# First loads on one queue, fillings by 0.7 of the wait, output transfers as steps of the plan, and new ranks in a two-layer attention kernel

## The chip, the cores and the metric

The kernel runs on one core of a Trainium2 chip. Its engines work side by side, each from its own queue of instructions in order: TensorE (matmuls; PE, and PEld for its weight loads), VectorE (DVE), ScalarE (ACT), GpSimd (POOL) and SyncE (SP), which only issues transfers. ScalarE and GpSimd can issue transfers too. Engines wait for one another by semaphores. The metric is the device time of one execution in microseconds; lower is better.

## The reference

`x` is 16 batch elements of 256 tokens and 256 features; `ctx` is 16 elements of 77 tokens. The first layer is a transformer block, the second a pair of attentions round a very narrow mlp (4 hidden units). All is float32.

```python
# layer 0: 16 heads of 16 features
h = rmsnorm(x, sa_w);   h = x + attention(h, h, sa_wq, sa_wk, sa_wv, sa_wo)
hn = rmsnorm(h, ca_w);  h = h + attention(hn, ctx, ca_wq, ca_wk, ca_wv, ca_wo)
hn = rmsnorm(h, mlp_w); h = h + (silu(hn @ w_gate) * (hn @ w_up)) @ w_down     # 256 -> 1024 -> 256

# layer 1: one head
nX, nF = layernorm(ctx, n1w, n1b), layernorm(h, n2w, n2b)
a = softmax(nF @ nX.T * 256 ** -0.5) @ nX
c = gelu(a @ fc1_w.T + fc1_b) @ fc2_w.T + fc2_b                                 # 256 -> 4 -> 256
n = layernorm(c, n3w, n3b)
out = nF + gamma2 * (c + gamma1 * (softmax(n @ n.T * 256 ** -0.5) @ n))
```

## The kernel before

A batch element's 256 tokens are two tiles of 128 partitions. Elements are loaded and stored in pairs (`UB = 2`, buffers `h`), the context in pairs too (`cx` for layer 0, `cx2` for layer 1). The work of one element is written as generators, one for each stage: `self_operands` (rmsnorm, feature-major copy, projections `psq`, `psk`, `psv`), `self_maxima` (scores `sc`, row maxima, their transposes `tm`), `exponentials` (scores again, transposed, as `st`, then the exponential `pT`), `outputs` (`po`), `projection` (`wo`), the same for the cross attention (`cross_queries` with `pscq`, `csc`, `cst`, `cpo`, `cwo`; `cross_keys` with `tpc` for a pair), `mlp` (`pg`, `pu`, `wd`), `second_context` and `second` for layer 1. Scores use TensorE in row groups of 32 partitions (shape "r"), attention outputs and `lav` in column groups of 32 (shape "c"), the rest the full array ("f").

To get features onto partitions, the first pair transposes on TensorE (`tp_sa`, `tp_ca`, `tp_mlp`). Later elements transpose blocks of 32 on VectorE (`hb`, L429), write them to DRAM (`blocks`, L434) and read them back re-arranged (`hnT`, L439); both transfers are issued by SyncE.

The order is written out by a planner at build time. Every generator yields `Step`s: TensorE's time (`pe`), its shape, the work of other engines that follows (`ops`), what it needs, which buffers it takes and frees, and a `lag`, the time by which what it gives becomes ready after it. `Order` holds a clock for each engine. In each turn `start` (L263) tells for each stream the earliest time of its next step. Among TensorE steps the one with the smallest key is chosen: first those that are not late, then by rank, which is the batch number plus a constant of the stage (`RANKS`, L1234; the second number is added for the first two elements, the third for the last three), plus a penalty for a change of shape (`STANDS_BACK`, L235) and for the wait. Steps without TensorE are put in between when they fit. `put` then makes the generator emit the instructions, so the order of the calls is the order in every engine's queue. Times of loads are given as constants (`order.done`, L1227).

When the chosen TensorE step starts later than TensorE's clock, `keep_busy` (L326) puts fillings there: `idle` matmuls of the identity on itself, in the shape of the moment, whose output is not used. Their number comes from the planned wait and `T_IDLE`; the first ones (`FIRST_IDLE`) stand at the start of the kernel.

The head of the kernel is issued in plain order before the plan: `h` of the first pair in four tiles (L102 to L105) with the context in between, then GpSimd's identity and the two halves of `sa_nw`, then on ScalarE's queue `wq`, `wk`, `wv` (two transfers each) and `wo`, and on SyncE's the second pair, the cross weights, the mlp weights (L156 to L165), the later pairs and the small constants of layer 1 (`second_constants`, L874). The weights `wq`, `wk`, `wv`, `cwq`, `wg`, `wu` are then multiplied by their norm's weights in place (L1209). The store of a finished pair (L1192) is issued right behind VectorE's last addition (L1191), whose step is also what frees the buffer of `h` in the plan.

## Time and profile before

| what | value |
|---|---|
| time, median of 3 runs | 997.14 us (995.62 to 997.92) |
| time of the profiled execution | 996.82 us |
| its span, first to last instruction | 995.0 us |
| mean granted TensorE clock | 0.989 |
| VectorE, ScalarE, GpSimd busy | 63%, 48%, 9% of the span |
| transfers | 39.61 MB, mean 40 GB/s; 275 GB/s in the first fortieth of the span |
| waits of TensorE, the three longest in sum | `tp_sa` for ScalarE 2.6 us, the first `idle` 2.5 us, `pscq` for the read-back of `hnT_ca` 2.4 us |
| SyncE waiting for VectorE's last addition before a store | 123.6 us, 8 times |

The span is the time between the first and the last instruction; 1.8 us of the profiled execution's time lie outside. "Busy" for TensorE has modelled ends, and fillings count as busy, so the share says that TensorE always had something to do, not that it was useful. Two records stand for one float32 matmul, for the matmul and for its weight load alike. A line of the timeline has start, duration, engine, source line, operation, what is written and read, and in brackets how long the engine was idle before and what ended it. In the table of stretches PEclk is the share of TensorE's full clock that was granted. Line numbers are those of the kernel before.

### The profile page before, as it was taken

Reading aid. Unit: us, or ns where it says so; the run is one execution under the profiler, and the core shown is the slowest. Engines: PE = TensorE matmul, PEld = TensorE weight load, DVE = VectorE, ACT = ScalarE, POOL = GpSimd, SP = SyncE. Lnnn points to the kernel's source line nnn. Section 1 sums busy time; section 2 is a strip of 40 time slices with the busy share of each in tenths; the row PEclk is TensorE's granted clock in tenths of the full one; section 3 lists DMA queues with packets and bytes.
Section 4 is the critical chain, followed back from the end, with each engine's and each line's share of the span. In section 5 each row is a group of like instructions: output and inputs, shape, how many; then the busy total and the mean of one; then the engine's idle time right before and its main releaser. Section 6 shows DMA issues by size and latency. Waiting matters only on the chain.

```text
span 995.0 us, 18977 instructions
## 1 busy us (share of the span) xinstructions
PE 968.8 (97%) x8136; PEld 715.0 (72%) x8136; DVE 622.7 (63%) x1075; ACT 475.7 (48%) x770; POOL 93.7 (9%) x124
## 2 busy tenths in 40 slices
PE   7989999999999999999999999999999999999997
PEld 6766666676776667777776777777677777778876
DVE  4865576666675657766676655775578565655552
ACT  4246645334555364543755354454571526543432
POOL 2510000000010010100100000010020000100210
PEclk9899999999999999999999999999999999999997
DMA  8301001001000111002100121011210110001000
GB/s 275 82 24 39 22 11 40 2 22 32 29 23 22 42 61 43 12 33 77 43 12 22 46 83 46 1 33 35 64 54 1 49 33 23 32 12 54 12 22 22
DMA packets 45732, 39.61 MB, mean 40 GB/s; under 512 B 4336, under 2 KB 39760, under 8 KB 45648
## 3 DMA queue, kind: packets, MB, share of 16 engines
q1 hardware_dynamic: 44448, 37.34, 11.8%
q8 instruction: 64, 1.05, 0.4%
q10 hardware_dynamic: 1136, 1.05, 0.3%
q14 instruction: 20, 0.16, 0.1%
q0 software_dynamic: 64, 0.00, 0.0%
HBM read 23.14 MB, written 15.20 MB: 39 GB/s over the span
## 4 chain that ended last, share of the span: by engine, by line
PE 86%; DMA 4%; DVE 4%; ACT 4%; issue 1%; ACTq 0%; POOL 0%; SPq 0%; POOLq 0%
PE pg L828 11%; PE pu L828 11%; PE wd L858 11%; PE sc L574 6%; PE st L635 6%; PE po L677 5%; PE cst L635 3%; PE psq L499 3%; PE pscq L499 3%; PE wo L716 3%; PE cpo L677 3%; PE cwo L716 3%; PE psk L499 3%; PE psv L748 2%; PE csc L600 2%; ACT pT L643 2%
## 5 line engine op out<-in xcount | busy, mean ns | idle before, releaser
L579 DVE TENSOR_REDUCE nmax<-sc 128x8 f32<-128x2048 f32 x64 | 146.6, 2290 | 39.3 <-PE sc L574 39.2
L643 ACT ACTIVATE pT<-st 128x2048 f32<-128x2048 f32 x64 | 120.1, 1877 | 100.9 <-PE st L635 100.7
L828 PE MATMUL pg<-hnT_mlp,wg 128*128 128x256 f32 x512 | 129.8, 387 | 0.0
L828 PE MATMUL pu<-hnT_mlp,wu 128*128 128x256 f32 x512 | 128.7, 387 | 0.5 <-DVE sg L839 0.5
L858 PE MATMUL wd<-wd,gT 128*128 128x256 f32 x512 | 126.3, 388 | 0.0
L828 PEld LDWEIGHTS pu<-hnT_mlp,wu 128*128 128x128 f32 x512 | 93.4, 190 | 22.9 <-issue 10.6
L858 PEld LDWEIGHTS wd<-wd,gT 128*128 128x128 f32 x512 | 92.6, 190 | 23.8 <-issue 11.9
L828 PEld LDWEIGHTS pg<-hnT_mlp,wg 128*128 128x128 f32 x512 | 92.6, 190 | 21.0 <-issue 9.5
L643 ACT ACTIVATE cpT<-cst 77x2048 f32<-77x2048 f32 x32 | 59.9, 1872 | 59.2 <-PE cst L635 59.2
L838 ACT ACTIVATE sg<-pg 128x512 f32<-128x512 f32 x64 | 38.2, 597 | 101.5 <-PE pg L828 101.3
L839 DVE SCALAR_TENSOR_TENSOR sg<-sg,pg 128x512 f32<-128x512 f32 x64 | 43.9, 686 | 67.2 <-ACT sg L838 66.7
L677 PE MATMUL po<-pT,vone 128*32 128x256 f32 x1024 | 62.7, 382 | 0.1
L840 DVE SCALAR_TENSOR_TENSOR gT<-sg,pu 128x512 f32<-128x512 f32 x64 | 43.7, 683 | 28.5 <-PE pu L828 27.4
L607 DVE TENSOR_REDUCE nmax<-csc 128x16 f32<-128x1232 f32 x32 | 46.1, 1440 | 8.3 <-PE csc L600 8.0
L677 PEld LDWEIGHTS po<-pT,vone 128*32 128x32 f32 x1024 | 29.7, 109 | 26.0 <-issue 9.7
L210 POOL TENSOR_TENSOR rstd_n<-ve_n,neg_half 128x4 f32<-128x4 f32 (+3 forms) x28 | 23.4, 837 | 206.2 <-DVE ve_n L208 160.6
L210 POOL TENSOR_TENSOR rstd_ca<-ve_ca,neg_half 128x2 f32<-128x2 f32 x16 | 11.1, 697 | 304.7 <-DVE ve_ca L208 304.6
L335 PE MATMUL idle<-ident 128*128 128x128 f32 (+2 forms) x198 | 32.5, 327 | 2.5 <-POOL ident masks.py:199 2.5
L499 PE MATMUL pscq<-hnT_ca,cwq 128*128 128x256 f32 x128 | 31.7, 388 | 2.4 <-DMA hnT_ca<-blocks_ca 2.4
L499 PE MATMUL psk<-hnT_sa,wk 128*128 128x256 f32 x128 | 33.4, 397 | 0.0
L499 PE MATMUL psq<-hnT_sa,wq 128*128 128x256 f32 x128 | 33.4, 399 | 0.0
L335 PEld LDWEIGHTS idle<-ident 128*128 128x128 f32 (+2 forms) x198 | 30.7, 228 | 3.5 <-POOL ident masks.py:199 2.5
(614 smaller groups left out, 1570.8 us busy)
## 6 DMA issues: line engine op xcount, KB each, us to landing
h<-in_x_dram SPq DMA_DIRECT2D x7, 512.0 KB
blocks_sa<-hb_sa SPq DMA_DIRECT2D x14, 256.0 KB
hnT_sa<-blocks_sa SPq DMA_DIRECT2D x14, 256.0 KB
blocks_ca<-hb_ca SPq DMA_DIRECT2D x14, 256.0 KB
hnT_ca<-blocks_ca SPq DMA_DIRECT2D x14, 256.0 KB
blocks_mlp<-hb_mlp SPq DMA_DIRECT2D x14, 256.0 KB
hnT_mlp<-blocks_mlp SPq DMA_DIRECT2D x14, 256.0 KB
out_dram<-h SPq DMA_DIRECT2D x7, 512.0 KB
```

The lines of the kernel that those rows point to most:

```text
L335: nc.tensor.matmul(ps[cols, :P], lhsT=ident[rows, cols], rhs=ident[rows], start=True, stop=True)
L499: nc.tensor.matmul(ps[:, m * n : (m + 1) * n], lhsT=w[:, c, m * P : (m + 1) * P], rhs=src(c), start=(c == 0), stop=(c == NC - 1),)
L574: nc.tensor.matmul(sc[:, j, (1 - e) * S : (2 - e) * S], lhsT=a.qx[rg, c, e, qt * P : (qt + 1) * P], rhs=a.kx[rg, c, e], start=True, stop=True,
L579: nc.vector.tensor_reduce(maxima_of(nm, qt)[:, :, c::NC], sc.rearrange("p j (y k) -> p j y k", y=2), AX.X, ALU.max, negate=True,)
L607: nc.vector.tensor_reduce(maxima_of(nm, qt), sc[:, :, : 2 * NC * SK].rearrange("p j (n k) -> p j n k", k=SK), AX.X, ALU.max, negate=True,)
L635: nc.tensor.matmul(st[:nk, j, e * S : (e + 1) * S], lhsT=a.kx[rg, c, e, kc * P : kc * P + nk], rhs=a.qx[rg, c, e], start=True, stop=True,)
L643: nc.scalar.activation(a.pT[k][:nk].rearrange("p j e q -> p j (e q)"), st[:nk], AF.Exp, scale=HD ** -0.5,)
L677: nc.tensor.matmul(po[RG * j : RG * (j + 1), e, :], lhsT=a.v[:nk, kc, 8 * c + 2 * j + e, :], rhs=pT[:nk, j, e, :], start=(kc == 0 and e == ...
L716: nc.tensor.matmul(ps[:, i * D : (i + 1) * D], lhsT=oT[:, c, i * P : (i + 1) * P], rhs=a.w[:, c, :], start=(c == 0), stop=(c == NC - 1),)
L828: nc.tensor.matmul(ps[:, i * S : (i + 1) * S], lhsT=w[:, c, (f + i) * P : (f + i + 1) * P], rhs=tokens_moving(hnT, c), start=(c == 0), sto ...
L839: nc.vector.scalar_tensor_tensor(sg, sg, 1.0, ps, ALU.add, ALU.mult)
L858: nc.tensor.matmul(ps[:, :D], lhsT=gT[:, f, i * P : (i + 1) * P], rhs=wd[:, f, :], start=(f == 0), stop=(f == NF - 1),)
```

## The change

The four tiles of the first pair, the context, `sa_nw`, `wk`, `wv` and `wo` are issued on SyncE in the order in which they are used; of the first weights `wq` alone stays on ScalarE. The fillings' number is 0.7 of the planned wait less 150 ns, over `T_IDLE`, from one filling up (before: the wait less 350 ns, from two up), and 9 instead of 12 at the start. A TensorE step is late from a wait of 200 ns (100), a wait weighs 0.003 per ns in its rank (0.05), late ones go by their start alone, and leaving row or column groups for the full array costs 50 ranks (5). Steps of SyncE that would begin after TensorE's clock are set aside until TensorE's clock has passed them or nothing else is left; other steps may run 800 ns past the chosen TensorE step (500). The store of a finished pair is a step of SyncE of its own, and the buffer of `h` is free 3 us after it. The planned times of first loads and contexts are new, and so are most of the `RANKS`.

```diff
-    for t in range(NT):
-        if t == QT:
-            cxs[0] = load_context(0, UB, "cx")
-        load_tokens(0, t)
...
+    for t in range(QT):
+        load_tokens(0, t)
     ident = const.tile([P, P], F32, tag="ident", name="ident")
     make_identity(nc, ident)
-    sa_nw = load_columns(sa_norm_w, "sa_nw", nc.gpsimd, True)
+
+    wq = load_matrix(sa_wq, "wq", nc.scalar, True)
+    sa_nw = load_columns(sa_norm_w, "sa_nw", nc.sync, True)
+    wk = load_matrix(sa_wk, "wk", nc.sync, True)
+    wv = load_matrix(sa_wv, "wv", nc.sync, True)
+    for t in range(QT, NT):
+        load_tokens(0, t)
+    cxs[0] = load_context(0, UB, "cx")
+    wo = load_matrix(sa_wo, "wo", nc.sync)
...
-    wq = load_matrix(sa_wq, "wq", nc.scalar, True)
-    wk = load_matrix(sa_wk, "wk", nc.scalar, True)
-    wv = load_matrix(sa_wv, "wv", nc.scalar, True)
-    wo = load_matrix(sa_wo, "wo", nc.scalar)
     load_tokens(1)
...
-    T_IDLE, FIRST_IDLE = 220, 12
+    T_IDLE, FIRST_IDLE = 220, 9
-    STANDS_BACK = {"rf": 5, "cf": 5, "fc": 10}
+    STANDS_BACK = {"rf": 50, "cf": 50, "fc": 10}
...
-            n = int((t - self.clock["P"] - 350) / T_IDLE) if self.clock["P"] else FIRST_IDLE
-            if n < 2 or None in bank + after or max(bank + after) > self.clock["P"]:
+            n = int((0.7 * (t - self.clock["P"]) - 150) / T_IDLE) if self.clock["P"] else FIRST_IDLE
+            if n < 1 or None in bank + after or max(bank + after) > self.clock["P"]:
                 return
...
-                        late = wait > 100
-                        rank = st.rank[0] + STANDS_BACK.get(turn, 0) + 0.05 * wait
-                        key = (late, t + T_TURN[turn] if late else 0, rank, st.rank[1])
+                        late = wait > 200
+                        rank = st.rank[0] + STANDS_BACK.get(turn, 0) + 0.003 * wait
+                        key = (late, t if late else 0, rank, st.rank[1])
...
-                        aux.append((max(t + T_NEXT, self.clock[e]), st.rank, st, t))
+                        b = max(t + T_NEXT, self.clock[e])
+
+                        (ahead if e == "S" and b > self.clock["P"] else aux).append(
+                            (b, st.rank, st, t)
+                        )
+                if not best and not aux:
+                    aux = ahead
                 if aux:
                     b, _, st, t = min(aux, key=lambda a: a[:2])
-                    if best is None or b + sum(o[1] for o in st.step.ops) <= best[2] + best[1].step.pe + 500:
+                    if best is None or b + sum(o[1] for o in st.step.ops) <= best[2] + best[1].step.pe + 800:
...
-        yield Step(460, "r", "sc", ops=[("V", 70 + 290 * NT)], rel=[("h", u)] * (first + nb == UB),
-                   gives=[("second", n)])
+        yield Step(460, "r", "sc", ops=[("V", 70 + 290 * NT)], gives=[("second", n)])
         nc.vector.tensor_tensor(h, h, by_rows(zT, k["last"], "out"), ALU.add)
+        yield Step(ops=[("S", 600)], rel=[("h", u)] * (first + nb == UB), lag=3000)
         nc.sync.dma_start(tokens(out, u)[:, first * QT : first * QT + NT], h)
...
     def context_loads():
...
-                ops=[("S", 100)], acq=[("cx", u)], gives=[("cx", u)], lag=4000 if u else 6000
+                ops=[("S", 100)], acq=[("cx", u)], gives=[("cx", u)], lag=(8000, 20000)[u] if u < 2 else 4000
...
     def second_loads():
...
-            yield Step(ops=[("S", 100)], acq=[("cx2", u)], gives=[("cx2", u)], lag=4000)
+            yield Step(ops=[("S", 100)], acq=[("cx2", u)], gives=[("cx2", u)], lag=4000 if u > 1 else 20000)
...
-        ("x", 0): 5e3, ("x", 1): 20e3, "wq in": 8e3, "wk in": 9e3, "wv in": 10e3, "cwk": 12e3,
+        ("x", 0): 4e3, ("x", 1): 20e3, "wq in": 5e3, "wk in": 6e3, "wv in": 7e3, "cwk": 12e3,
...
     RANKS = {
...
-        "outputs": (6.5, -1, 50),
-        "exponentials": (-52.5, -50, 4),
-        "projection": (-0.5, -50, -0.5),
-        "cross_outputs": (5, 0, 0.25),
-        "cross_exponentials": (-100, 0, 0),
-        "cross_projection": (-50.5, 0, 50),
-        "self_maxima": (-0.25, -50, -100),
-        "cross_maxima": (-49, 0, 0),
-        "cross_queries": (-2, 1, -49.5),
-        "self_operands": (-2, 0, -0.5),
-        "cross_keys": (1.75, 0, 0),
-        "mlp": (4.25, 2.75, -2.5),
-        "second_context": (5.5, 0, -50),
-        "second": (3, 0, -50),
+        "outputs": (5.5, -1, 50),
+        "exponentials": (-51.5, -50, 5),
+        "projection": (0.5, -50, 3.5),
+        "cross_outputs": (-45, 0, 0.25),
+        "cross_exponentials": (-50, -50, 0),
+        "cross_projection": (-51.5, 0, 50),
+        "self_maxima": (0, -50, -50),
+        "cross_maxima": (-50, 0, -50),
+        "cross_queries": (-1, -52, 0.5),
+        "self_operands": (0, 0, -50.5),
+        "cross_keys": (2.25, 0, 48),
+        "mlp": (5, -0.25, 47.5),
+        "second_context": (-44.5, 0, 0),
+        "second": (-48, -1.5, -50),
```

More of the change, by code (lines that the diff above doesn't have):

```diff
@@ L342, in run @@
                 best = None
-                aux = []
+                aux, ahead = [], []
                 for st in self.streams:
```

## The prediction

> **What bounds the kernel now.** I read the page first: shares, then the 40 slices.
>
> ```profile
> PE 968.8 (97%) x8136; PEld 715.0 (72%) x8136; DVE 622.7 (63%) x1075; ACT 475.7 (48%) x770; POOL 93.7 (9%) x124
> PE   7989999999999999999999999999999999999997
> PEclk9899999999999999999999999999999999999997
> ```
>
> TensorE is the bound in every slice but the first four and the last. No other engine comes near, so what counts is TensorE's time without real work: waits, fillings, a halved clock. The table by stretches puts it in place (length; busy us of PE, PEld, DVE, ACT, POOL; clock; DMA share; GB/s):
>
> ```profile
> 34.90:41.70 6.80, 6.80 (x40) 5.98 (x39) 4.08 (x5) 0.00 (x0) 2.62 (x2) 0.50 0.31 103
> 41.70:125.00 83.30, 77.43 (x798) 54.61 (x796) 51.59 (x82) 49.04 (x76) 7.34 (x19) 1.00 0.08 26
> 125.00:965.00 840.00, 834.13 (x6988) 614.36 (x6988) 538.00 (x915) 402.70 (x642) 65.49 (x78) 1.00 0.10 33
> 970.20:980.40 10.20, 9.74 (x45) 8.40 (x42) 4.30 (x18) 2.56 (x5) 1.18 (x2) 0.50 0.08 27
> ```
>
> From 125 to 965 us only 5.9 of 840 us are idle. The clock halves twice: after the start, and in the tail. The same table for the fillings (`idle`) alone, PE's and PEld's busy time:
>
> ```profile
> 41.00:125.00 84.00, 10.18 (x80) 9.66 (x80) 1.00 0.08 26
> 965.00:995.00 30.00, 10.55 (x58) 9.82 (x58) 0.76 0.05 18
> ```
>
> Each `idle` matmul is two instructions. From 41 to 125 us there are 10.2 us of fillings and 83.3 - 77.4 = 5.9 us idle: some 16 us without real work. The timeline of the start shows what is late first:
>
> ```profile
> 0.75 1.28 ACTq L116 DMA_DIRECT2D wq<-in_L_xattn_sa_wq_dram  x2
> ...
> 6.98 0.41 ACTq L120 DMA_DIRECT2D wo<-in_L_xattn_sa_wo_dram  x1
> 7.42 1.28 ACT L377 ACT_TABLE_LOAD   x1 [7.42 <-DMA wv<-in_L_xattn_sa_wv_dram]
> ...
> 8.71 0.42 ACT L377 ACTIVATE sq_sa<-h 128x256 f32<-128x256 f32 x1
> ...
> 13.26 2.05 PE L499 MATMUL psq<-hnT_sa,wq 128*128 128x256 f32 x8
> ```
>
> ScalarE issues seven loads before its first table load, so the first square starts at 8.71 and the first projection 4.55 us after it.
>
> **The change part by part.** Sums stand against the profiled execution: span 995.0, own time 996.82, which is 0.3 below the median of 997.14.
>
> *First loads.* ScalarE keeps two of seven issues (1.28 us); its table load moves from 7.42 to about 2.1, and ends by 3.4. The tiles of `h` keep their place at the head of SyncE's queue, issued at 0.74 and 1.18; the two small loads on GpSimd, issued at 1.29 and 2.39, are the nearest rows with a landing, 4.45 and 6.75: 3.2 to 4.4 us. So the squares can start at about 4.2 and the projection at 4.2 + 4.55 = 8.8. But SyncE now issues, one after another, two tiles of `h`, two of `sa_nw`, two each of `wk` and `wv`, two more of `h`, and only then the context, which was third: with rows of 0.43, 0.6, 0.63 and 0.43 us that is 0.74 + 0.9 + 1.2 + 2.5 + 0.9 = 6.2, landing 3.2 later at 9.4. Its transposes (`tpc`, L765) stand ahead of `psq` in TensorE's order and take 0.4. So `psq` at 9.9, a lead of 3.4 us (2 to 4.5). GpSimd sheds 1.3 us of issuing, which nothing waits for.
>
> Here a rule can be held against the trace. The Trainium skill, "DMA: Bandwidth & Descriptors", section "Issuing engines are not separate DMA queues", says that issuing from several engines saves only the sequencer's time, usually small beside the transfer. By the rule the move is worth about nothing in either direction; by the rows the seven issues, with their waits, held ScalarE for 6.6 us in front of its first work. I go by the rows for the head. For what follows the rule holds: all loads share the transfer engines, and the bytes are the same. What is late next is the end of the loads:
>
> ```profile
> 32.80 0.25 PE L897 MATMUL tp_fc<-ident,fc_sb 4*128 4x4 f32 x2 [0.64 <-DMA fc_sb<-in_L_xattn_fc_w_dram]
> ...
> 33.10 0.17 DVE L900 COPY fc1T<-tp_fc 128x8 f32<-128x8 f32 x1 [0.27 <-PE tp_fc L897]
> 33.18 0.70 DVE L429 STREAM_TRANSPOSE hb_sa<-hn_sa 128x512 f32<-128x512 f32 x1
> ...
> 34.46 0.35 SPq L434 DMA_DIRECT2D blocks_sa<-hb_sa  x1
> ...
> 37.53 0.39 SPq L439 DMA_DIRECT2D hnT_sa<-blocks_sa  x1
> ...
> 41.05 2.31 PE L499 MATMUL psq<-hnT_sa,wq 128*128 128x256 f32 x8
> ```
>
> The constants land at about 32.7, behind all weights; VectorE's transpose of batch element 2 stands behind the copy that needs them; the round trip through DRAM stands behind their issues on SyncE. In the new order the constants are still behind all weights, and VectorE's transpose still behind their copy. So the third `psq` stays at about 41 (41 to 42.5, SyncE having seven more issues early), whatever the head gained. The lead is lost there except for what TensorE now does ahead of that `psq`: the first `st` block, 1.1 us with 0.35 of change-over. I take -1.4 (-3.4 if the constants land earlier too, +0.5 if `psq` slips to 42.5).
>
> *Fillings.* Built, the kernel has 64 `idle` matmuls instead of 99: 9 + 1 at the head (12 + 5 + 3), 4 + 2 before the third `psq` (10), 4, 3, 1, 5, 3 from there to the mlp of element 0 (12, 4, 3, 4, 8, 4, 3, 2), one in the middle, and 31 in the tail (29). Between 29 and 41 us TensorE now has only about 5 us of work and six fillings. The Trainium skill, "TensorE: Matmul & The Clock Gate", Part 1, says that the clock is halved by default, comes back after about 3.4 us of sustained work and falls after an idle window; this speaks against fewer fillings. The trace agrees on the fall (0.50 from 34.9), but not that a full queue is enough: the 20 instructions of fillings from 34.7 to 38.7 used 32 rows, and the clock stayed at 0.50 to 41.7. Going by the rule alone, fewer fillings cost a window at each long wait; by the trace, one fall stands there already. It should now last one window longer, into dense work after 41: 3.4 us at half speed, +1.7 (0 to +3.4).
>
> From 41 to 125 a filling of n stands for a planned wait of about (220 n + 150) / 0.7 ns: 1.5, 1.2, 0.5, 1.8, 1.2, together 6.1 and below 7.7 us. With 3 us that I allow for waits too short to fill that is 10 us instead of 16: -6 (-2 to -9). What fills the rest is the mlp of element 0: by the last `st` block of element 2, 24 matmuls of `pg` and `pu` stand in TensorE's order, before none; at 0.43 us each 10.4 us of work moved forward.
>
> *Ranks and tolerance.* That work is missing later as cover. Also a step may now wait 200 ns, not 100, before it counts as late, and a wait weighs 0.003 instead of 0.05 in its rank, so short waits, for which no filling is put out, are taken in the middle stretch. Where a round trip through DRAM is planned tightly, its real length shows: twice 1.2 us before `pscq` in the table of waits. The trace can't show the new ones. Below, they can save no more than the 5.9 us idle there; above, they can give back all 6 us and one or two more stalls: -1 to +8. I take +4.5, nearer to giving back, since the matmuls are a fixed stock.
>
> *Change-overs between row groups, column groups and the full array* are 498 instead of 497: full to row 202 (204), row to full 176 (177), row to column 41 (38), column to full 44 (46), full to column 19 (20), column to row 16 (12). At the medians of the trace's gaps, 0.09 us into row or column and 0.25 to 0.26 for the other kinds, that is -0.2 - 0.25 + 0.76 - 0.5 - 0.1 + 1.0: +0.7.
>
> *Transfers put out in their time.* The output step now goes on SyncE's queue by its due time, and the buffer of `h` comes free 3 us after it. Behind it stand the next load of `h` and round trips. SyncE waited 123.6 us for VectorE's last add before outputs, but TensorE's waits name no output and only 2.4 us of round trips. Nothing, with -1 to +1 for a round trip that moves in front or behind.
>
> *The tail.*
>
> ```profile
> 975.50 6.15 PE L335 MATMUL idle<-ident 128*128 128x128 f32 x32
> ...
> 978.84 0.25 DVE L1113 COPY mga<-mg 128x12 f32<-128x12 f32 x2
> ...
> 981.48 0.27 PE L1124 MATMUL tp_g2T<-ident,g 128*64 128x128 f32 x1
> ```
>
> At half clock 16 fillings took 6 us (0.37 each) and held `tp_g2T` back by some 2.3 us after its input. Twelve take 4.5 at half clock, 2.7 at full: 1.5 to 2.3 saved. Against that `out` of element 14 now stands ahead of `xsc` and can hold it up by 0.8. I take -1.3 (-2.3 to +0.8).
>
> The sum: -1.4 + 1.7 - 6 + 4.5 + 0.7 - 1.3 = -1.8, so 995.0 on the profiled execution and 995.3 against the median.
>
> **The rivals.** *The middle doesn't give back*: 41 to 125 us pays its 6 and the middle at most 0.5, 995.3 - 4 = 991.3. For it speaks that 125 to 965 had little waiting before; against it, the work moved forward. *The loads were no wall*: constants land as much earlier as the head starts, 2 more, 993.3; against it, equal bytes. *All is hidden*: the head is lost at 41 us, the middle gives back its 6, the tail stays at half clock with 0.5 saved: -1.8 + 1.5 + 0.8 = +0.5, 997.6. *Slower, by the clock*: between 41 and 125 us fillings held 1.00; with 16 for 40 of them, the clock falls there. Each fall of 6.8 us (the row above) on dense work costs 3.4. One fall past 1.8 / 3.4 of its length turns the sign; two make 995.3 + 6.8 = 1002.1.
>
> **How the numbers follow.** Likeliest 0.40, its own range 993.3 to 997.3; no giving back 0.18; no wall 0.07; hidden 0.15; clock 0.20. A measurement of this kernel tells about 0.2% (2 us) from no change: faster ends at 995.1, slower begins at 999.1. The likeliest case is half faster and half same; the first two rivals are faster but for 0.03; hidden is same; the clock case is slower but for 0.02. Faster 0.42, same 0.40, slower 0.18. Left out: a tenth above 1001 (two falls and more), a tenth below 990.5 (middle and wall both).
>
> **What would show it.** First square near 4.2 and `psq` near 10; third `psq` still at 41 to 42; granted clock 0.50 somewhere between 31 and 46; `idle` from 41 to 125 near 3.6 us and PE idle there near 6; idle from 125 to 965 near 10; `tp_g2T` of the last element less than 1 us behind its `mga`. I am wrong if the third `psq` comes before 39, if the clock falls after 50 us, or if the middle's idle time stays under 7 or passes 14.

## The result and the profile after

The changed kernel takes 996.86 us (median of 14 executions, 994.79 to 999.13), the kernel before 996.69 us beside it (14 executions, 991.87 to 999.88). The ratio is 1.0004, 95% interval 0.9989 to 1.0019: no difference that can be measured. The profiled execution took 995.75 us for a span of 994.0 (before: 996.82 for 995.0). Executions of one kernel lie up to 8 us apart here, so the 1.1 us between the two profiled ones proves nothing; what the traces are good for is the place of things.

The page of the changed kernel, its shares and its 40 slices:

```profile
PE 963.3 (97%) x8066; PEld 706.0 (71%) x8066; DVE 623.1 (63%) x1075; ACT 475.1 (48%) x770; POOL 91.9 (9%) x122
PE   7899999999999999999999999999999999999997
PEclk8799999999999999999999999999999999999998
```

Seventy fewer TensorE records, all of them fillings (35 of two records each); the clock row dips in the first two slices, before in the second alone. What it shows of the first few microseconds is no reading, though: the first record of the clock is at 4.8 us (before: 7.6), and up to there the fillings go at half the pace that they have behind it, 13 records in 2.9 us against 6 in 0.6:

```profile
1.80:4.70 2.90, 2.89 (x13) 2.89 (x14) 1.00 0.66 200
4.80:5.40 0.60, 0.60 (x6) 0.50 (x5) 1.00 0.51 133
```

So both kernels start at half clock, over nothing but fillings. Busy time by stretches (length; PE, PEld, DVE, ACT, POOL; clock; DMA share; GB/s):

```profile
8.20:15.00 6.80, 5.37 (x16) 4.30 (x16) 0.41 (x5) 2.90 (x9) 0.95 (x2) 0.50 0.89 285
35.50:49.10 13.60, 11.49 (x75) 6.79 (x75) 7.72 (x16) 4.24 (x6) 0.69 (x1) 0.50 0.17 54
41.00:125.00 84.00, 79.97 (x761) 54.33 (x757) 53.17 (x87) 47.84 (x80) 5.62 (x9) 0.95 0.08 26
125.00:965.00 840.00, 829.66 (x6975) 611.34 (x6976) 533.52 (x908) 403.47 (x641) 65.10 (x77) 1.00 0.10 33
```

And of the fillings alone, PE and PEld:

```profile
41.00:125.00 84.00, 5.51 (x36) 5.07 (x36) 0.95 0.08 26
125.00:965.00 840.00, 0.99 (x6) 0.98 (x6) 1.00 0.10 33
```

From 41 to 125 us TensorE is idle for 84 - 79.97 = 4.0 us and fills for 5.5: 9.5 us without real work. Before, the same stretch had 5.9 idle and 10.2 filled, 16.1:

```profile
41.00:125.00 84.00, 78.13 (x800) 55.21 (x798) 52.29 (x82) 49.04 (x76) 7.34 (x19) 1.00 0.08 26
```

From 125 to 965 us the changed kernel is idle for 10.3 us (5.9 before). So 6.5 us are won in the first stretch and 5.5 (4.5 idle, 1.0 filled) given back in the second. The clock is at one half for 6.8 us where it was not before, and for 13.65 us at the place where it had been for 6.8.

The start, as a timeline:

```profile
3.33 0.42 ACT L384 ACTIVATE sq_sa<-h 128x256 f32<-128x256 f32 x1
...
6.70 0.43 SPq L99 DMA_DIRECT2D cx<-in_ctx_dram  x1
...
9.69 0.74 PE L772 MATMUL tpc<-ident,cx 77*128 77x77 f32 x4 [1.43 <-DMA cx<-in_ctx_dram]
...
10.23 3.71 PE L506 MATMUL psq<-hnT_sa,wq 128*128 128x256 f32 x8
```

The first square starts at 3.33 instead of 8.71. The context, now behind ten other issues on SyncE, lands last of what the first `psq` stands behind, and `tpc` waits for it. The first `psq` comes 3.0 us earlier (10.23, before 13.26) but takes 3.71 us instead of 2.05, since the clock has halved at 8.2. By the first scores the lead is 0.8 us (19.03, before 19.83).

The loads' end and the third batch element:

```profile
33.30 2.29 DVE L586 TENSOR_REDUCE nmax<-sc 128x8 f32<-128x2048 f32 x1 [1.19 <-PE sc L581]
...
33.86 0.28 PE L904 MATMUL tp_fc<-ident,fc_sb 4*128 4x4 f32 x2 [0.63 <-DMA fc_sb<-in_L_xattn_fc_w_dram]
...
35.50 0.16 DVE L907 COPY fc1T<-tp_fc 128x8 f32<-128x8 f32 x1
35.58 0.70 DVE L436 STREAM_TRANSPOSE hb_sa<-hn_sa 128x512 f32<-128x512 f32 x1
...
40.62 2.09 PE L642 MATMUL st<-qx__228,kx__239 32*128 32x256 f32 x16 [1.96 <-DVE nmax L586]
...
42.49 1.06 PE L336 MATMUL idle<-ident 32*128 32x128 f32 x4
...
43.48 2.08 PE L506 MATMUL psq<-hnT_sa,wq 128*128 128x256 f32 x4
```

The constants still come late, but what `hb_sa` stands behind is now a row maximum of 2.29 us on VectorE. The third `psq` starts at 43.48 (before 41.05), and its line shows no idle time in front of it: it does not wait for its read-back, TensorE only gets to it then, behind a row maximum, scores at half clock (2.09 us; 1.15 at full clock) and two fillings.

The tail:

```profile
977.12 2.92 PE L336 MATMUL idle<-ident 128*128 128x128 f32 x24
980.19 0.30 PE L1131 MATMUL tp_g2T<-ident,g 128*64 128x128 f32 x1
...
980.70 0.25 DVE L1120 COPY mga<-mg 128x12 f32<-128x12 f32 x2
```

Twelve fillings take 2.92 us at full clock, and `tp_g2T` no longer waits for them: it runs ahead of `mga` instead of 2.4 us behind its end. The clock falls 15.7 us after the start of the last `wd`, before it fell 5.3 us after it. The last `wd` starts 3.9 us later than before (968.73, before 964.81), and the kernel ends 1.0 us earlier.

Counting each real matmul at its steady pitch in the traces (820 us in all) gives an estimate, good to about 1 us, of how far the kernel is at a given time. The changed kernel is level at 41 us, 2.7 us behind at 60 us, 3.4 ahead at 125, 5.2 at 200, 3.2 at 300, 1.6 at 500, 0.7 at 900. What it wins early it loses in the middle: of the 4.5 us of more idle time 3.0 lie between 200 and 500 us.

### The profile page after: what moved, and what is told of

The parts are those of the page before. It is cut to its first block, busy times and chain, and to the rows that moved or that the text cites. A ratio compares the mean times of both kernels' runs of the same rounds, so it can differ in the third digit from the quotient of the medians.

```text
span 994.0 us, 18845 instructions
## 1 busy us (share of the span) xinstructions
PE 963.3 (97%) x8066; PEld 706.0 (71%) x8066; DVE 623.1 (63%) x1075; ACT 475.1 (48%) x770; POOL 91.9 (9%) x122
## 4 chain that ended last, share of the span: by engine, by line
PE 80%; DVE 9%; ACT 6%; DMA 2%; issue 2%; SPq 1%; POOL 0%; POOLq 0%; ACTq 0%; DVEq 0%
PE pu L835 10%; PE wd L865 10%; PE pg L835 10%; PE st L642 6%; PE sc L581 6%; PE po L684 5%; DVE nmax L586 3%; PE psq L506 3%; PE pscq L506 3%; PE cst L642 3%; PE wo L723 3%; PE psk L506 3%; PE cpo L684 3%; PE psv L755 3%; PE cwo L723 2%; PE csc L607 2%
## 5 line engine op out<-in xcount | busy, mean ns | idle before, releaser
L835 PEld LDWEIGHTS pu<-hnT_mlp,wu 128*128 128x128 f32 x512 | 93.1, 190 | 23.4 <-issue 10.3
L506 PE MATMUL psq<-hnT_sa,wq 128*128 128x256 f32 x128 | 37.4, 420 | 0.3 <-DMA hnT_sa<-blocks_sa 0.3
L870 DVE TENSOR_TENSOR h<-h,wd 128x256 f32<-128x256 f32 x32 | 13.3, 417 | 33.9 <-PE wd L865 33.8
L755 PE MATMUL psv<-wv,hnT_sa 128*128 128x256 f32 x128 | 32.6, 389 | 0.0
L211 POOL TENSOR_TENSOR rstd_mlp<-ve_mlp,neg_half 128x2 f32<-128x2 f32 x16 | 11.1, 695 | 229.1 <-DVE ve_mlp L209 229.1
```

Of the source, the lines that this page charges most:

```text
L506: nc.tensor.matmul(ps[:, m * n : (m + 1) * n], lhsT=w[:, c, m * P : (m + 1) * P], rhs=src(c), start=(c == 0), stop=(c == NC - 1),)
L755: nc.tensor.matmul(ps[:, t * D : (t + 1) * D], lhsT=tokens_still(hnT, c)[:, t * P : (t + 1) * P], rhs=wv[:, c, :], start=(c == 0), stop=(c ...
L835: nc.tensor.matmul(ps[:, i * S : (i + 1) * S], lhsT=w[:, c, (f + i) * P : (f + i + 1) * P], rhs=tokens_moving(hnT, c), start=(c == 0), sto ...
```

## The experiments

Every kernel computes the whole reference. Ratios are to the kernel before, run beside it on the same chip, with 95% intervals from 4 to 22 executions. Four theories were at stake: that the new order, the new head (the first loads) and the new filling numbers each have a sign of their own; that the clock takes the head's lead; that the loads' end is a wall; and that the new tolerance lets waits into the middle.

**The parts one by one**

*The new order alone* (head, filling rule and stores as before):

```diff
+    for t in range(NT):
+        if t == QT:
+            cxs[0] = load_context(0, UB, "cx")
+        load_tokens(0, t)
...
+    sa_nw = load_columns(sa_norm_w, "sa_nw", nc.gpsimd, True)
...
+    wq = load_matrix(sa_wq, "wq", nc.scalar, True)
+    wk = load_matrix(sa_wk, "wk", nc.scalar, True)
+    wv = load_matrix(sa_wv, "wv", nc.scalar, True)
+    wo = load_matrix(sa_wo, "wo", nc.scalar)
...
-    T_IDLE, FIRST_IDLE = 220, 9
+    T_IDLE, FIRST_IDLE = 220, 12
...
-            n = int((0.7 * (t - self.clock["P"]) - 150) / T_IDLE) if self.clock["P"] else FIRST_IDLE
+            n = int((t - self.clock["P"] - 350) / T_IDLE) if self.clock["P"] else FIRST_IDLE
...
-        yield Step(ops=[("S", 600)], rel=[("h", u)] * (first + nb == UB), lag=3000)
```

> Changed kernel with the old head of loads, the old filling rule and the old place of the stores: TensorE's order of real matmuls is that of the changed kernel, so this is the new plan alone. Theory of exchange (work of the mlp is pulled into early waits, and the middle gives it back): the stretch 41 to 125 us holds about 5 us more real work than in the kernel before, 125 to 900 us has about 5 us more waiting, and the time is within 2 us of before. Rival (the new plan is the loss, and head and fillings made up for it): 2 to 4 us slower than before. Rival (the plan is the gain and fewer fillings ate it): 2 to 4 us faster than before, with the clock at half for 7 us instead of 20 in the first 50 us.

Measured: 1000.20 us, 1.0044 (1.0030 to 1.0058). The third `psq` came at 45.76 (before 41.05), and the clock was at one half from 10.5 to 17.3, 41.2 to 51.5 and 116.3 to 123.1. The new order by itself loses 4 us.

*The new head alone, in the old order*:

```diff
-    sa_nw = load_columns(sa_norm_w, "sa_nw", nc.gpsimd, True)
+    wq = load_matrix(sa_wq, "wq", nc.scalar, True)
+    sa_nw = load_columns(sa_norm_w, "sa_nw", nc.sync, True)
+    wk = load_matrix(sa_wk, "wk", nc.sync, True)
+    wv = load_matrix(sa_wv, "wv", nc.sync, True)
+    for t in range(QT, NT):
+        load_tokens(0, t)
+    cxs[0] = load_context(0, UB, "cx")
+    wo = load_matrix(sa_wo, "wo", nc.sync)
```

> Kernel before with the new head of loads alone; TensorE's order and fillings are those of before. Theory of the wall (the constants' loads decide when the third psq can start): first psq at 10 to 11 instead of 13.3 us, third psq still at 40.5 to 42, time within 1.5 us of before. Rival (the lead is kept where nothing else is changed): third psq at 38 to 39, time 2 to 3 us below before.

Measured: 1000.87 us, 1.0041 (1.0029 to 1.0052). In the old order `tpc` is TensorE's first work, and it waits for the context that is now issued late:

```profile
10.34 0.78 PE L766 MATMUL tpc<-ident,cx 77*128 77x77 f32 x4 [3.52 <-DMA cx<-in_ctx_dram]
...
15.27 2.07 PE L500 MATMUL psq<-hnT_sa,wq 128*128 128x256 f32 x6
...
41.11 2.50 PE L500 MATMUL psq<-hnT_sa,wq 128*128 128x256 f32 x5 [0.23 <-DMA hnT_sa<-blocks_sa]
```

The first `psq` is 2.0 us later than before, though ScalarE has long been ready. But this delay is not the 4 us: at the third `psq` the kernel is level with the one before (41.11 and 41.05), although `hb_sa` is 2.1 us later (35.29). TensorE's order is the same in both, so the traces can be laid side by side: this execution loses 1.0 us at half clock behind the third `psq`, 1.5 where the clock falls again at 74.4 us, 1.5 about a wait of `pscq` at 836.5 and 0.9 in the tail. Why the head leads to these is open.

*The new filling numbers alone, in the old order* and only where it has fillings already:

```diff
+            n = int((0.7 * (t - self.clock["P"]) - 150) / T_IDLE) if self.clock["P"] else 9
```

> Kernel before with the new numbers of fillings at the places where it has fillings already; order and loads are those of before. Theory of the clock: the first 50 us lose 1 to 3 us to a longer stretch at half clock, the tail gains 1.5 to 2 because tp_g2T of the last element comes less than 1 us after its input, together within 1.5 us of before. Rival (fillings only delay): no longer half clock, tail gain kept, 1.5 to 3 us faster than before.

Measured: 993.56 us, 0.9971 (0.9960 to 0.9982). It is the one part that gains by itself, though not mainly where its fillings stand. In the tail twelve fillings instead of sixteen let `tp_g2T` start 1.2 us after `mga`'s copy began instead of 2.6, again with most of them at half clock:

```profile
972.54 4.73 PE L336 MATMUL idle<-ident 128*128 128x128 f32 x24
975.88 0.25 DVE L1114 COPY mga<-mg 128x12 f32<-128x12 f32 x2
977.11 0.27 PE L1125 MATMUL tp_g2T<-ident,g 128*64 128x128 f32 x1
```

That is 1.0 of the 4.4 us between the profiled executions. From 41 to 125 us the kernel is without real work for 16.2 us, as long as the one before. 2.7 us lie between 160 and 230 us, where neither kernel has a filling. There the kernel before waits twice for a read-back, at 169.6 and 225.9 us:

```profile
PE pscq L499 <- DMA hnT_ca<-blocks_ca: 2.4, 2, 1.2
```

Here both waits are missing. The three traces of the old order with the smaller numbers have 0 to 0.6 us of them, the four with the old numbers 1.3 to 2.4; why is open.

*The changed kernel with the old head, and with the old filling rule*: the same edits, taken back one at a time.

> Changed kernel with the old head of loads; order, filling rule and stores are the changed ones. The plan alone (order only) cost 4.4 us, and the new filling numbers alone took 2.9 us off the kernel before. If the parts add up, this is 1.5 us slower than before (998 with before at 996), and the new head is worth 1 us in the new order. If the head is what carries the new order (its context's transposes stand behind the first pair's transposes, as the loads come in), this is 3 to 4 us slower than before, and the third psq starts at 45 to 46 instead of 43.5.

Measured: 1000.91 us, 1.0046 (1.0027 to 1.0066). In the new order the old head costs 4 us:

```profile
14.34 3.71 PE L504 MATMUL psq<-hnT_sa,wq 128*128 128x256 f32 x8
...
47.32 2.07 PE L504 MATMUL psq<-hnT_sa,wq 128*128 128x256 f32 x4
```

Against the changed kernel the first `psq` is 4.1 us later and the third 3.8: within one order the head's lead goes through the third `psq` whole. In this execution 2.6 us more were lost where the clock fell, from 117.6 to 124.4 us.

> Changed kernel with the old filling rule; order, head and stores are the changed ones. If the parts add up, it is 3 us slower than the changed kernel (3 us slower than before), 1.5 to 2 us of that in the tail, where 16 fillings instead of 12 stand ahead of tp_g2T, which then comes over 2 us after its input. If the filling rule matters only for the clock at the head, the tail is the same and the time moves by less than 1 us.

Measured: 996.31 us, 0.9999 (0.9981 to 1.0017). The expected loss in the tail is missing: at full clock 16 fillings take 3.8 us, and `tp_g2T` comes on time with them as well:

```profile
975.79 3.82 PE L336 MATMUL idle<-ident 128*128 128x128 f32 x32
...
979.36 0.25 DVE L1120 COPY mga<-mg 128x12 f32<-128x12 f32 x2
979.44 0.27 PE L1131 MATMUL tp_g2T<-ident,g 128*64 128x128 f32 x1
```

So in the new order it is the clock, not the number of fillings, that relieves the tail. In the seven traces of the old order, with whatever fillings, it falls 3.0 to 5.3 us after the start of the last `wd`; in five of the seven of the new order 15.7 to 16.3 us after it. The other two, 3.7 and 4.1 us after it, are the ones with more fillings at the start and with the old rules for choosing a step, below. From 41 to 125 us this kernel is without real work for 84 - 80.90 + 6.46 = 9.6 us, as long as the changed one (the second row is its fillings):

```profile
41.00:125.00 84.00, 80.90 (x770) 55.33 (x766) 53.16 (x87) 48.29 (x80) 5.63 (x9) 0.95 0.08 26
41.00:125.00 84.00, 6.46 (x46) 6.02 (x46) 0.95 0.08 26
```

So those 6.5 us come from the order (the first `pg` is at 117.0 instead of 126.3), not from shorter fillings.

The parts do not add. With the ratios to the kernel before:

| | old head | new head |
|---|---|---|
| old order | 1 | 1.0041 |
| old order, new filling numbers | 0.9971 | not tried |
| new order, old filling rule | 1.0044 (old stores) | 0.9999 |
| new order, new filling rule | 1.0046 | 1.0004 |

Order and head fit each other: either one alone costs 4 us, together they cost and gain nothing. The new order asks for `tp_sa` before `tpc`, and the new head brings `h` and the weights before the context; that this is the whole reason is not shown, and for the old order a run below speaks against it.

**The clock at the start**

*More fillings of the full array in the first 45 us of the changed kernel*:

```diff
-    T_IDLE, FIRST_IDLE = 220, 9
+    T_IDLE, FIRST_IDLE = 220, 14
...
+            early = self.clock["P"] < 38e3
+            if 0 < self.clock["P"] < 9e3:
+                n = 7
+            spare = None in bank + after or max(bank + after) > self.clock["P"]
+            if n < 1 or spare and not early:
                 return
...
+            if early:
+                rows = cols = slice(P)
...
```

> Changed kernel with more fillings in its first 45 us only, all on 128 rows: 14 instead of 9 at the start, 7 and 7 instead of 1 round the context's transposes, 4 where there were 4, 5 and 6 new ones in the two waits before the third psq that had none (into the bank of the attention outputs, not yet in use). The order is that of the changed kernel. Theory of the clock (its two halvings at 8 to 15 and 35.5 to 49 us cost real time): no half clock after 5 us, first sc at 17 instead of 19.0, the third psq at 41.5 instead of 43.5, 3 to 5 us faster than the changed kernel, so 992 to 994. Rival (VectorE's maxima and the round trip through DRAM set the pace there, whatever the clock): less than 1 us.

Measured: 994.63 us, 0.9985 (0.9972 to 0.9997). The clock, from its first record at 7.2 us on, stayed full to 72 us, and the third `psq` came at 40.85, but only some 2 us were gained instead of the 3 to 5 expected, at the edge of what the two intervals tell apart. The clock then fell in dense work:

```profile
5.00:40.00 35.00, 32.13 (x255) 26.59 (x254) 22.22 (x40) 12.71 (x30) 15.65 (x19) 1.00 0.81 233
72.10:75.50 3.40, 3.29 (x24) 2.13 (x28) 0.05 (x1) 2.33 (x4) 0.00 (x0) 0.51 0.43 147
109.70:116.30 6.60, 6.60 (x46) 5.10 (x43) 3.70 (x4) 1.91 (x4) 0.48 (x1) 0.50 0.00 1
```

So the halved clock did take part of the head's lead: at 60 us this execution is 4.9 us ahead of the changed kernel's. It then loses 1.2 and 2.6 us where the clock fell, 10.2 us in all at half speed on nothing but real work, and 3.3 in the tail, where the clock fell 3.7 us after the start of the last `wd`.

**The wall**

*The new head in the old order with the context third*, so that `tpc` need not wait:

```diff
+    for t in range(QT):
+        load_tokens(0, t)
+    cxs[0] = load_context(0, UB, "cx")
...
-    cxs[0] = load_context(0, UB, "cx")
```

> Kernel before with the new head of loads, but with the context third on SyncE's queue as before, because its transposes stand first in the old order. Theory: the 4 us that the new head cost in the old order came from that one transfer alone; with it third, tpc starts at 5 to 7 instead of 10.3 and the first psq at 9 to 10.5 instead of 15.3. With the wall of the constants the third psq still starts at 40 to 41 and the time is within 1 us of before. Without a wall: third psq at 37 to 38.5 and 2 to 3 us faster than before. If serial issue on SyncE is itself the loss, tpc is early and the time is still 3 us above before.

Measured: 1001.89 us, 1.0051 (1.0036 to 1.0067). The start did what it should: first `psq` at 10.47, first scores 2.8 us earlier than before. Then the second pair's context was not there, and VectorE stood empty for 3.4 us before the copy of the constants:

```profile
31.82 0.75 PE L766 MATMUL tpc<-ident,cx 77*128 77x77 f32 x4 [3.13 <-DMA cx<-in_ctx_dram]
...
33.46 0.17 DVE L901 COPY fc1T<-tp_fc 128x8 f32<-128x8 f32 x1 [3.42 <-PE tp_fc L898]
```

```profile
31.60:45.00 13.40, 12.54 (x68) 10.43 (x69) 7.36 (x10) 1.34 (x5) 3.11 (x3) 0.50 0.20 56
```

TensorE ran at half clock for 13.65 us behind that wait, twice as long as before, and the third `psq` came at 42.53. The lead ended later than no lead. That is 1.5 us of the 6.3 between the profiled executions; 0.9 follow at half clock, 1.5 at a fall of the clock at 75.8 us, 1.6 about a wait of `pscq` at 837.4 and the rest in the tail, at the same places as with the new head alone. So in the old order the late issue of the first context was not what cost the 4 us.

*The same, with the load of `wd` (1 MB, used after 125 us only) issued some 15 us later*, which takes its bytes out of the first 32 us:

```diff
-    wd = load_matrix(w_down, "wd", nc.sync)
+    wd = const.tile([P, w_down.shape[0] // P, D], F32, tag="wd", name="wd")
...
+        nc.sync.dma_start(wd, w_down.rearrange("(c p) n -> p c n", p=P))
         nc.sync.dma_start(last[H5:HZ, :], gg)
```

> The kernel before with the new head and the context third, and beside it the 1 MB load of wd (used after 125 us only) issued some 15 us later, at the constants' last step instead of in the head; TensorE's order and fillings stay. In the kernel with the context third alone, the second pair's tpc waited 3.1 us for its context at 31.8 us and VectorE stood empty 3.4 us before the copy of tp_fc, so the third psq came at 42.53 and the clock was half from 31.5 to 45.1. Theory 1 (the bytes of the first loads are the wall; the late context and the halved clock behind the wait ate the lead): tpc without a wait, hb_sa some 3 us earlier, third psq at 39 to 40, half clock no longer than one window of 7 to 10 us, time 994 to 998. Theory 2 (what costs is the serial issue on SyncE): tpc gains less than 1 us, third psq stays above 42, time within 1.5 us of 1001.9.

Measured: 998.30 us, 1.0017 (0.9999 to 1.0035), 0.34% below the run without that edit; the two intervals just do not touch.

```profile
28.80 0.46 PE L766 MATMUL tpc<-ident,cx 77*128 77x77 f32 x4 [0.99 <-DMA cx<-in_ctx_dram]
...
38.82 2.91 PE L500 MATMUL psq<-hnT_sa,wq 128*128 128x256 f32 x8 [2.83 <-DMA hnT_sa<-blocks_sa]
```

`hb_sa` is 3.3 us earlier, the third `psq` 3.7, and the clock is at one half for 3.4 us there instead of 13.65. Theory 1 holds in the old order: with fewer bytes in front of them the context and the constants come earlier, and now the third `psq` does wait for its read-back (2.83 us). At 60 us this execution is 3.2 us ahead of the one without the edit; how much of it is the loads and how much the halved clock behind the wait is not told apart. The time itself ends just above what theory 1 gave.

*The changed kernel with `wd` later*, the same edit:

> The changed kernel with the load of wd issued some 15 us later; TensorE's order stays. In the changed kernel tp_fc waited 1.0 us for fc_sb at 33.86, but hb_sa (35.58) stood behind a row maximum of 2.3 us on VectorE. Theory 1 (in the new order VectorE's row maxima, not the loads, set the third psq): tp_fc at about 33.2, third psq at 42.5 to 43.5, time 995 to 997.5. Theory 2 (the loads' bytes are the wall, as the prediction had it): third psq at 40.5 to 41.5 and half clock shorter by a window, time 992 to 994.5.

Measured: 998.42 us, 1.0009 (0.9997 to 1.0021). `tp_fc` no longer waits, but stands in TensorE's order behind scores that wait for VectorE, and `hb_sa` stands behind the next row maximum:

```profile
32.54 2.29 DVE L586 TENSOR_REDUCE nmax<-sc 128x8 f32<-128x2048 f32 x1 [1.19 <-PE tp_fc L904]
...
34.82 0.70 DVE L436 STREAM_TRANSPOSE hb_sa<-hn_sa 128x512 f32<-128x512 f32 x1
```

The third `psq` is at 41.92, between what the two theories gave, and the time, above both, does not improve. Of the 1.6 us at the third `psq` 0.75 were there by 20 us already, ahead of the constants. Again the line of the third `psq` has no wait for the read-back. In the new order the loads are a small part of what sets it; scores and their row maxima in turn are what TensorE has in front of it. The 1.8 us that this execution was ahead at 150 us went mostly at two falls of the clock, at 381.7 and 849.3 us.

**The tolerance**

*The changed kernel with the old rules for choosing a step*:

```diff
-    STANDS_BACK = {"rf": 50, "cf": 50, "fc": 10}
+    STANDS_BACK = {"rf": 5, "cf": 5, "fc": 10}
...
-                        late = wait > 200
-                        rank = st.rank[0] + STANDS_BACK.get(turn, 0) + 0.003 * wait
-                        key = (late, t if late else 0, rank, st.rank[1])
+                        late = wait > 100
+                        rank = st.rank[0] + STANDS_BACK.get(turn, 0) + 0.05 * wait
+                        key = (late, t + T_TURN[turn] if late else 0, rank, st.rank[1])
```

> The changed kernel with the old rules for choosing a step (late from 100 ns, 0.05 rank per ns, late ones by start and change-over, penalty 5 for leaving row or column groups); ranks, head, filling rule and stores stay new. Theory 1 (the tolerance lets short waits into the middle, as the prediction said): idle time of TensorE from 125 to 965 us falls from 10 to 6 or 7 us, but change-overs rise by 20 or more, at 0.2 us each 4 us, so the time is 994 to 1000. Theory 2 (the middle's idle time comes from the mlp work moved forward, whatever the rule): idle time stays at 9 us or more, and the time is 998 to 1003.

Measured: 1023.05 us, 1.0266 (1.0240 to 1.0292). Both theories fall.

```profile
41.00:125.00 84.00, 78.52 (x687) 53.85 (x686) 48.68 (x81) 44.03 (x75) 5.63 (x9) 0.87 0.09 29
125.00:965.00 840.00, 820.15 (x6919) 598.30 (x6918) 527.45 (x879) 398.87 (x631) 62.65 (x74) 1.00 0.10 33
```

The middle's idle time doubles to 19.9 us, and by 125 us the kernel is by the same estimate some 8 us of work behind the changed one. The new ranks are good only under the new rule. Since ranks and rule don't fit here, the run does not show how much of the idle time that the changed kernel has more in the middle is the tolerance's.

**Better versions**

*The old order and head, with smaller filling numbers after the first 20 us and fillings of the full array up to 45 us*:

```diff
+            if self.clock["P"] > 20e3:
+                n = int((0.7 * (t - self.clock["P"]) - 150) / T_IDLE)
+            if self.clock["P"] < 45e3:
+                rows = cols = slice(P)
```

> Kernel before with its own fillings in the first 20 us, the new, smaller numbers behind them, and full-array fillings up to 45 us; order and loads are those of before. Theory: the gain of the new numbers (2.9 us) comes from fillings that no longer outlast their wait, mainly the tail's, and the half clock at 10 to 17 us that the shorter head cost is avoidable: 3 to 5 us faster than before, no half clock before the tail. Rival (the head's fillings only delayed, the shorter head was the gain): 1 to 2 us faster than before.

Measured: 991.63 us, 0.9952 (0.9938 to 0.9966), 0.5% below the kernel before. The clock did fall before the tail, from 42.7 to 46.1 us, behind a wait of 2.39 us for the read-back at the third `psq` (42.17).

*The same with the new head, the context third and `wd` later*:

> The old order with everything that the runs so far point to: new head with the context third, wd later, the first twelve fillings and those of the first 20 us by the old rule, smaller numbers after that, and full-array fillings up to 45 us. Theory 1 (the head's lead counts if neither the loads nor the clock take it back): third psq at 39 to 40, no halved clock longer than 7 us before 60 us, time 987 to 990.5, that is 0.6 to 1.0% below the kernel before. Theory 2 (the lead is lost in any case at VectorE's queue): third psq at 41 or later, time 991 to 993, as with the fillings alone; theory 3 (serial issue on SyncE costs 4 to 5 us however it is arranged): 995 to 997.

Measured: 992.60 us, 0.9954 (0.9938 to 0.9970). The mechanism of theory 1 is there, its time is not:

```profile
37.45 1.85 PE L504 MATMUL psq<-hnT_sa,wq 128*128 128x256 f32 x7 [0.52 <-DMA hnT_sa<-blocks_sa]
```

The third `psq` is 3.6 us ahead of the kernel before, and so is what follows: the first `pg` is at 122.4 (before 126.3), the last `wd` at 958.5 (before 964.8). Yet the median is that of the version with the old head. The profiled execution of that version was its slowest (996.43 of 990.16 to 996.43), so its trace can't show where it makes good the difference; that stays open.

## Why the prediction came out as it did

The likeliest case said 995.3 (-1.8 against the profiled execution), within 993.3 to 997.3; measured are 996.86 and no difference. Its two large terms, 41 to 125 us and the middle, came out and cancelled as it said. That the whole sum held is luck: the head and the half clock behind it came out 3.4 us worse than predicted, and what is left for change-overs and tail 3.2 better. By its steps, in us:

| step | predicted | measured |
|---|---|---|
| first square, first `psq` | 4.2, 9.9 | 3.33, 10.23 |
| third `psq` | 41 to 42.5 | 43.48 |
| head, to 41 us | -1.4 | about 0, level in real work |
| half clock behind it, after 41 us | +1.7 | (8.2 - 0.7) / 2 = +3.7 |
| 41 to 125 us, time without work | -6 | -6.5 |
| middle | +4.5 | +5.5 |
| change-overs and tail | +0.7 - 1.3 = -0.6 | about -3.8 |
| sum | -1.8 | -1.1 between the profiled executions, +0.2 between the medians |

The last measured term is what is left of -1.1 after the others, so it takes in their errors.

*First loads.* Right in the mechanism up to `psq`: the first square moved by 5.4 us and `tpc` waited for the late context. The move's worth was mis-sized. The step took the clock as full behind it, where the nine first fillings ended at about 5.5 us; 6.8 us at half speed began at 8.2, which no term of the sum had, and the lead of 3.0 us at `psq` was 0.8 at the first scores. The rule of the Trainium skill quoted there, that issuing from several engines saves only a sequencer's time and little, gives a move of about nothing. That is the sum of order and head together, but for another reason: under the new order the head's place is worth 4 us (1.0046 against 1.0004), under the old order it costs 4.

*The wall.* Against the kernel before, the lead is gone at the third `psq`, as predicted, but not by the wall that was predicted. In the new order the head's 3.8 us go through it whole (43.48, with the old head 47.32); what takes them away is the order, whose third `psq`, with the old head and the old fillings, is at 45.76. Nor does that `psq` wait for the end of the chain that was named, constants, transpose, read-back: its line has no idle time in front of it, in the changed kernel and, as the prediction's own row shows (41.05, no bracket), in the one before. TensorE stands there behind scores, row maxima and fillings at half clock. With the clock full the third `psq` comes at 40.85 in the new order, and in the old one at 41.11 although `hb_sa` is 2.1 us later. So "41 to 42.5" was too early by 1 us mainly because of the half clock (2.6 us between 43.48 and 40.85); `wd` out of the way is worth 1.6 us. As a limit the loads showed only in the old order with the context third, where the same edit brought `psq` from 42.53 to 38.82.

*The half clock behind the wall.* Predicted was one window more, 3.4 us, "+1.7 (0 to +3.4)". It lasted 13.65 us instead of 6.8, two windows more, and 8.2 us of it lay behind 41 us. This and the head's are the terms that were mis-sized. The Trainium skill ("TensorE: Matmul & The Clock Gate", Part 1) speaks against fewer fillings here, by one window at each long wait; the prediction let the trace of before outweigh it for lack of a stretch like this. The runs side with the rule in direction (full clock to 72 us with more fillings), but give it 2 us, not one window for each wait.

*Fillings and work moved forward.* -6.5 against -6, but the cause is half of what was said: with the old filling rule the same stretch is without work for 9.6 us, so it is the order with its mlp moved forward. In the old order the smaller numbers save nothing there either (16.2 us); they do gain in time (0.9971), by 1.0 us in the tail and mostly where no filling stands, at two read-backs of the middle.

*The middle.* +5.5 against +4.5, so it is given back, as "the matmuls are a fixed stock" says. That the missing mlp is the reason was argued, not tested. The tolerance, named there as what lets the waits in, was neither shown nor cleared: taking it back under the new ranks doubled the waits.

*Change-overs, stores, tail.* The tail gained, and `tp_g2T` came ahead of `mga`. But fewer fillings, which were to bring it, are not the cause: sixteen of them are on time too, since under the new order the clock is full there. No term had that. The stores were not undone alone; nothing in TensorE's waits names them.

*The rivals.* "No wall" and "the middle doesn't give back" did not happen. "All is hidden" has the time nearest to the median (997.6), but not its mechanism: the tail was not at half clock at `tp_g2T`, and more than 0.5 us was gained there. The slower rival named the right cause, the clock, at the wrong place: behind the wall, not after 50 us; it was wrong for this kernel and in part right for the new order without its head, where the clock fell from 117.6 to 124.4 us and took 2.6 us, beside the 3.8 that were lost from the start.

## What to carry to other kernels

A part of a change that was tuned together with others has no worth of its own: loads in the order of use are worth 4 us to the order that uses them so and cost 4 us to another. Ahead of any gain at the start, look for what really ends last at the next point that all must pass: a late transfer whose reader shows no wait is not what holds it up (here TensorE came to the third `psq` late, behind row maxima and scores at half clock). Count the halved clock as part of a wait's price. Work moved forward to fill waits is missing later; credit it only where the later stretch has other cover.

## What the runs showed of the hardware that was not expected

The clock falls even deep in dense work, and TensorE's busy time alone does not tell when. Ahead of the last `wd` the fourteen traces have 29 falls. In front of 23 of them TensorE was busy for 2.5 us or less of 3.4; in front of the other six, for 2.7 to 3.4. The wait of the same scores for a row maximum of VectorE, 1.24 us, stands in the changed kernel and in the one with `wd` later, which have the same order. In the changed kernel the clock stays full; in the other it falls for 3.4 us:

```profile
381.00:384.40 3.40, 2.16 (x24) 1.52 (x23) 3.40 (x6) 0.00 (x0) 0.00 (x0) 1.00 0.03 5
```

```profile
378.30:381.70 3.40, 2.16 (x23) 2.00 (x26) 3.40 (x4) 0.90 (x2) 0.11 (x1) 1.00 0.00 0
381.80:385.00 3.20, 3.20 (x18) 1.86 (x11) 3.17 (x6) 0.62 (x2) 0.00 (x0) 0.50 0.00 0
```

The stretches before the falls at 34.9 us of the kernel before, and at 8.2 and 35.5 us of the changed one, were busy for 2.19, 1.73 and 1.95 of 3.4 us. But the first row below, of the changed kernel, is no busier and has no fall behind it, and the second, of the new head in the old order, is almost full and stands right in front of one:

```profile
264.00:267.40 3.40, 1.98 (x32) 1.16 (x35) 1.23 (x4) 3.10 (x4) 0.20 (x2) 1.00 0.00 0
```

```profile
71.00:74.40 3.40, 3.35 (x40) 3.12 (x36) 3.40 (x4) 0.00 (x0) 0.00 (x0) 1.00 0.00 0
74.50:77.80 3.30, 3.30 (x17) 2.22 (x10) 0.64 (x3) 2.14 (x2) 0.00 (x0) 0.50 0.21 79
```

At 849 us of the run with `wd` later, too, the clock fell with no idle time before it that the trace shows. Halved stretches that the end does not cut last 3.4, 6.8, 10.2, 13.65 or 17.1 us. Whether a wait of about a microsecond brings a fall was different from one execution to another at the same place, and a fall of 3.4 us costs up to 1.7. That this is what spreads executions of one kernel over 5 to 8 us fits, but was only argued. The read-backs through DRAM are a rival: between traces of the old order the start of the same `pscq` moves by up to 1.8 us at one wait.
